# A quarter of a projection step behind the transposes in two attention slots, a whole step ahead of them in the third

## The chip, the cores and the metric

The kernel runs on one core of a Trainium2 chip. The metric is device time in microseconds (us) for one execution, and the number compared is the median over several executions. All data are float32.

## The reference, cut to what matters

Two layers follow each other on x of shape (16, 256, 512), with a condition of shape (16, 512). Each has a residual connection.

```python
# layer 1: adaptive norm, then attention with 16 heads of 32
scale, shift = split(cond @ W_emb + b_emb)
xn = rms_norm(x, g_norm) * (1 + scale) + shift
q, k, v = split_heads(xn @ W_qkv)              # 512 -> 3 * 512
q, k = rms_norm(q, g_q), rms_norm(k, g_k)
o = softmax(q @ k.T * 32 ** -0.5) @ v          # for each of 16 heads
x = x + o + o @ W_out
# layer 2: a GRU over the 256 time steps, started from cond
x = x + gru(x, h0=cond, W_ih, W_hh, b_ih, b_hh)
```

The change touches the attention of layer 1 only, and no arithmetic in it.

## The kernel before, in words

The program is unrolled. First come the weights and the projections of batch 0, then attention for 16 batches, then 256 steps of the GRU. An attention batch is worked off in four **slots**, one for each group of four heads. `slot0` to `slot3` run for batches 0 to 14, so that each of them runs 15 times. Batch 15 has a function of its own, `last_batch`, without projections.

A slot is a software pipeline over three things: the logits and softmax of the current group `w`, the transposes and the product with v of the previous group `prev`, and, spread over the four slots, all projections of the next batch `m = b + 1`. The names in the code and in the profile go like this:

- `logits` (L312, tile `lg`): 8 matmuls into four PSUM banks `lg0` to `lg3`, one bank a head.
- `project(b, n, s, ks, a)` (L244, tile `qkv`): one of q, k, v (s = 0, 1, 2) for one half of the tokens (n). It sums over four **steps** k. A step is four matmuls, j = 0 to 3. The matmul j has 32 columns of stationary operand (32 tokens) and writes 32 of the 128 partitions of the bank `a`; the moving operand is always the same 512 columns of the weights. In the trace each of these float32 matmuls stands as two records, one behind the other, so that a step is 8 records of PE.
- `maxima` (L328, DVE), `exps` (L334, ACT), `normalize` (L342 on DVE, L345 on POOL): the softmax of `w`. `exps` reads the four `lg` banks.
- `turn(prev)` (L218, tile `tpa`): 32 transposes of the previous group's attention weights, back into the four `lg` banks as soon as `exps` has read them.
- `put_turned(prev, "vava")` (L374, tile `attnT`): the copies of these four banks into SBUF, two by DVE and two by ACT in turn.
- `weigh(prev, bank)` (L391, tile `o`): 8 matmuls, four heads i for each of two halves k of the keys. Head i writes partitions 32 i to 32 i + 31. Heads 0 and 1 need the first two copies, heads 2 and 3 the other two.
- `turn_x` (L218, `tpx`), in slot 0, and `turn_qk` (L218, `tpqk`), twice in slot 3: transposes of the same shape as `tpa`, 16 each. `turn_qk` goes into the banks Z and Y.
- `norm_qk` (L273, DVE, tile `qkn`), `put_qk` (L296 on DVE, L294 on ACT), `put_v` (L267, ACT), `put_weighed` (L402, tile `oT`, ACT).

Under `manual_schedule` PE, DVE, ACT and POOL run their instructions in the order in which the code issues them. What sets the times is this order on each engine, with semaphores between the engines. So the place of a `project` call in a slot's code is its place in PE's queue. On PE, the four slots before the change are:

```
slot 0: logits, 4 steps, tpx, tpa, 2 steps, o
slot 1: logits, 5 steps, tpa, 1 step, o
slot 2: logits, 5 steps, tpa, 1 step, o
slot 3: logits, 4 steps, tpqk, tpa, tpqk, 2 steps, o
```

In slot 3 the first `tpqk` goes into the banks Z and Y, which hold q and k of the other half of the tokens until `norm_qk(m, 1, ...)` on DVE has read them; that follows the slot's `maxima` on DVE.

Of the kernel before, what the change touches and what calls it, by code (L numbers as in the profile page):

```python
# [19 lines left out]
def kernel(  # L20
# [125 lines left out]
    def tile_ps(name, bank, shape=(P, D)):  # L146
        pool = ps if len(bank) == 1 else ps_lg
        return pool.tile(list(shape), F32, tag=bank, name=name)
# [31 lines left out]
    def norm_first(b, parts=range(NT)):  # L180
        if parts[0] == 0:
            batches[b].ssx = small.tile([P, NT], F32, tag="ssx", name=f"ssx_{b}")
            batches[b].rs = Rsqrt(batches[b].ssx, D, NT, f"x{b}")
            if b != 2:
                batches[b].xs = p1.tile([P, NT, D], F32, tag="xs", name=f"xs_{b}")
        for n in parts:

            squares = batches[b].xs[:, n, :] if b != 2 else spare(f"squares_{n}")
            nc.scalar.activation(
                squares, x_tiles[b][:, n, :], AF.Square,  # L190
                accum_out=batches[b].ssx[:, n : n + 1],
            )
# [42 lines left out]
            else:  # L235
                nc.vector.tensor_scalar(dst, tps[r][:, c], a, s, ALU.mult, ALU.add)  # L236

    def project(b, n, s, ks, a):

        if isinstance(a, str):  # L240
            a = tile_ps(f"qkv_{b}_{n}_{s}", a)
        for k in ks:
            for j in range(4):
                nc.tensor.matmul(  # L244
                    a[32 * j : 32 * j + 32, :],
                    batches[b].xnT[:, k, n * P + 32 * j : n * P + 32 * j + 32],
                    wq[:, k, s * D : (s + 1) * D],
                    start=(k == 0),
                    stop=(k == KC - 1),
                )  # L250
        return a
# [17 lines left out]
    def norm_qk(b, n, accs, rstd):  # L269
        out = []  # L270
        for s in range(2):
            qk = p1.tile([P, H, DH], F32, tag="qkn", name=f"qkn_{b}_{n}_{s}", bufs=4)
            nc.vector.tensor_tensor(  # L273
                qk,
                accs[s].rearrange("p (h d) -> p h d", d=DH),
                rstd[:, s * H : (s + 1) * H].unsqueeze(2).to_broadcast([P, H, DH]),
                ALU.mult,
            )
            out.append(qk.rearrange("p h d -> p (h d)"))
        return out  # L280

    def turn_qk(b, n, normed, banks):
        tps = [tile_ps(f"tpqk_{b}_{n}_{r}", banks[r], (P, 2, NG, QR)) for r in range(R)]
        for s in range(2):
            for c in range(NG):
                turn_block([tp[:, s, c, :] for tp in tps], normed[s][:, c * P : (c + 1) * P])
        return tps
# [38 lines left out]
    def maxima(w, heads):  # L326
        for i in heads:
            nc.vector.tensor_reduce(w.neg[:, i, :], w.lg[i], AX.X, ALU.max, negate=True)  # L328

    def exps(w, heads):  # L330
        for i in heads:
            a = p1.tile([P, NT, T], F32, tag="attn", name=f"attn_{w.b}_{w.g}_{i}", bufs=8)
            for n in range(NT):
                nc.scalar.activation(  # L334
                    a[:, n, :], w.lg[i][:, n, :], AF.Exp,
                    bias=w.neg[:, i, n : n + 1], accum_out=w.den[:, i, n : n + 1],
                )
            w.attn[i] = a

    def normalize(w, heads=range(HG), engine=nc.gpsimd):  # L340
        r = slice(heads[0], heads[-1] + 1)
        nc.vector.reciprocal(w.rden[:, r, :], w.den[:, r, :])  # L342
        for i in heads:
            for n in range(NT):
                engine.tensor_scalar(  # L345
                    w.attn[i][:, n, :], w.attn[i][:, n, :], w.rden[:, i, n : n + 1], 1.0,
                    ALU.mult, ALU.mult,
                )
# [15 lines left out]
    def turn(w, banks=("lg0", "lg1", "lg2", "lg3")):  # L364

        if w is None:
            return
        for pair in range(HG // R):
            turn_pair(w, pair, banks[R * pair : R * pair + R])

    def put_turned_bank(w, i, engine):
        h, r = i // R * R, i % R
        dst = w.attnT[:, h : h + R].rearrange("p h k (n r c) -> p h k n r c", n=NT, r=R)[:, :, :, :, r]
        (nc.scalar.copy if engine is nc.scalar else nc.vector.tensor_copy)(dst, w.turned[i])  # L374

    def put_turned(w, engines):

        if w is None:
            return
        for i, e in enumerate(engines):  # L380
            put_turned_bank(w, i, nc.scalar if e == "a" else nc.vector)

    def weigh(w, bank):
        if w is None:
            return
        v = batches[w.b].v
        w.o = tile_ps(f"o_{w.b}_{w.g}", bank, (P, T))
        for k in range(NT):
            for i in range(HG):
                h = w.g * HG + i  # L390
                nc.tensor.matmul(  # L391
                    w.o[i * DH : (i + 1) * DH, :],
                    v[:, k, h * DH : (h + 1) * DH],
                    w.attnT[:, i, k, :],
                    start=(k == 0),
                    stop=(k == NT - 1),
                )

    def put_weighed(w, engine=nc.scalar):
        if w is None:  # L400
            return
        (nc.scalar.copy if engine is nc.scalar else nc.vector.tensor_copy)(oT[:, w.g, :, w.b], w.o)  # L402
# [56 lines left out]
    def slot1(b, w, prev, st):  # L459
        m = b + 1  # L460
        project(m, 0, 1, (2, 3), st.k)
        st.q1 = project(m, 1, 0, (0, 1, 2), "Z")
        maxima(w, range(HG))
        exps(w, range(HG))
        sq = st.s0.square(1, st.k)
        turn(prev)
        put_turned(prev, "vava")
        project(m, 1, 0, (3,), st.q1)
        st.s0.add(1, sq)
        if b + 3 < B:  # L470
            norm_first(b + 3, (0,))
        st.s0.rs.first()
        st.s1 = Stats(m, 1)
        st.sq = st.s1.square(0, st.q1)
        weigh(prev, "Y")
        put_weighed(prev)
        st.rstd = st.s0.rs.second()
        normalize(w)

    def slot2(b, w, prev, st):  # L480
        m = b + 1
        k = project(m, 1, 1, range(KC), "Y")
        maxima(w, range(HG))
        st.qk0 = norm_qk(m, 0, (st.q, st.k), st.rstd)
        st.v0 = project(m, 0, 2, (0,), "A")
        exps(w, range(HG))
        st.s1.add(0, st.sq)
        sq = st.s1.square(1, k)
        turn(prev)
        put_turned(prev, "vava")  # L490
        project(m, 0, 2, (1,), st.v0)
        st.s1.add(1, sq)
        if b + 3 < B:
            norm_first(b + 3, (1,))
        st.s1.rs.first()
        if b + 3 < B:
            batches[b + 3].rs.first()
        weigh(prev, "X")
        put_weighed(prev)
        if b == 0:  # L500

            for c in range(KC):
                d = wo[:, c, c * P : (c + 1) * P]
                nc.vector.tensor_tensor(d, d, ident, ALU.add)
            load_small()
        elif b == 2:
            for i in range(2):
                a = b_rows[:, 2 * i, :]
                nc.vector.tensor_tensor(a, a, b_more[:, i, :], ALU.add)
        st.accs = (st.q1, k)  # L510
        st.rstd = st.s1.rs.second()
        normalize(w)

    def slot3(b, w, prev, st):
        m = b + 1
        project(m, 0, 2, (2, 3), st.v0)
        st.v1 = project(m, 1, 2, (0, 1), "X")
        maxima(w, range(HG))
        qk1 = norm_qk(m, 1, st.accs, st.rstd)
        tq0 = turn_qk(m, 0, st.qk0, "ZY")  # L520
        if b + 3 < B:
            rstd = batches[b + 3].rs.second()
        exps(w, range(HG))
        put_qk(0, 0, tq0, nc.vector)
        put_qk(0, 1, tq0, nc.scalar)
        put_v(m, 0, st.v0)
        turn(prev)
        put_turned(prev, "vava")
        tq1 = turn_qk(m, 1, qk1, "ZY")
        project(m, 1, 2, (2, 3), st.v1)  # L530
        put_qk(1, 0, tq1, nc.vector)
        put_qk(1, 1, tq1, nc.scalar)
        if b + 3 < B:
            norm_apply(b + 3, rstd)
        normalize(w)
        weigh(prev, "A")
        put_weighed(prev)
        if m == B - 1:
            put_v(m, 1, st.v1)
# [89 lines left out]
    with tc.manual_schedule(engines=ORDERED):  # L629

        nc.scalar.preload_act_table_set("natural_log_exp_and_others")
        st = Batch()
# [236 lines left out]
    with tc.manual_schedule(engines=ORDERED):  # L869
# [7 lines left out]
        for c in (slice(0, 2 * B), slice(2 * B, TI * B)):  # L877
            for i, o in enumerate(first):
                a = xTs[0][:, 2 * i : 2 * i + 2].rearrange("p q t b -> p q (t b)")[:, :, c]
# [8 lines left out]
        for t in range(T):  # L888
            tl = t % TG
            p, s = divmod(t, 2)  # L890
# [18 lines left out]
            n = tile_of("n")  # L909
# [80 lines left out]
```

## Time and profile before

| what | value |
|---|---|
| median of 3 executions (lowest, highest) | 1746.63 us (1745.31, 1748.65) |
| the profiled execution's own time | 1746.58 us |
| its span, first to last instruction | 1744.8 us |
| granted TensorE clock, mean | 0.994 |
| PE busy | 1728.0 us, 99% of the span |
| DVE, ACT, POOL busy | 1051.4, 740.3, 315.5 us |
| projections L244 on PE | 354.7 us busy, 3072 records of 596 ns on average |
| slot 2 (236.87 to 245.56 us) | 8.69 us, PE busy 8.69 |
| slot 3 (245.56 to 255.63 us) | 10.07 us, PE busy 10.06 |
| slot 0 (255.63 to 264.74 us) | 9.11 us, PE busy 9.11 |
| slot 1 (264.74 to 273.49 us) | 8.75 us, PE busy 8.75 |

The last four rows are stretches of the trace from one slot's first projection to the next slot's. They are four consecutive slots in the middle of the attention part. A record of PE begins when the array takes the matmul, but its end is modelled and overlaps the next ones, so a "busy" PE can hold waits: what is read below are starts, and the length of a group of records from its first start to its last end. PEld is the loading of stationary operands, which runs beside the matmuls.

### The profile page before, as it was taken

The page shows a single profiled execution, that of the slowest core. Times are in us where ns is not written, and L with a number is a line of the kernel's source. Part 1 is how long each engine was busy: PE and PEld are TensorE (multiplying, and loading weights), DVE is VectorE, ACT ScalarE, POOL GpSimd, SP SyncE. Part 2 cuts the span into 40 slices and gives each one's busy share as a digit, 9 for nine tenths or more (in the row PEclk, how much of TensorE's full clock was granted, in tenths as well). Part 3 has the DMA queues.
Part 4 walks back from the last instruction along what each step waited for, and adds up shares of the span by engine and source line. Part 5 has one row for each costly group of instructions (what it writes and reads, how often), then busy time and mean ns, then how long its engine had stood idle before and what let it go on. Part 6 is the DMA issues. An engine that isn't in the chain of part 4 may idle for free.

```text
span 1744.8 us, 95656 instructions
## 1 busy us (share of the span) xinstructions
PE 1728.0 (99%) x42866; PEld 1272.0 (73%) x42866; DVE 1051.4 (60%) x3312; ACT 740.3 (42%) x2694; POOL 315.5 (18%) x773
## 2 busy tenths in 40 slices
PE   8999999999999999999999999999999999999998
PEld 4444444444444589888888888888888888888886
DVE  4777777777776645555555555555555555555554
ACT  4777777777777722222222222222222222222222
POOL 0443344334433410000000000000000000000000
PEclk9999999999999899999999999999999999999999
DMA  9100000000000310000000000000000000000000
GB/s 281 46 14 14 14 26 14 14 14 14 14 2 2 74 28 22 16 17 22 23 16 16 23 22 17 16 22 23 16 16 22 23 16 17 16 10 11 10 17 15
DMA packets 50506, 44.37 MB, mean 25 GB/s; under 512 B 10195, under 2 KB 43327, under 8 KB 50095
## 3 DMA queue, kind: packets, MB, share of 16 engines
q1 hardware_dynamic: 49959, 38.21, 8.3%
q8 instruction: 336, 5.51, 1.3%
q14 instruction: 75, 0.61, 0.1%
q10 hardware_dynamic: 136, 0.04, 0.0%
HBM read 29.79 MB, written 8.39 MB: 22 GB/s over the span
## 4 chain that ended last, share of the span: by engine, by line
PE 95%; DVE 2%; ACT 1%; issue 1%; DMA 0%; POOL 0%; SPq 0%; DVEq 0%; ACTq 0%
PE gr L808 25%; PE qkv L244 19%; PE gz L808 18%; PE gn L808 13%; PE o L765 6%; PE lg L312 4%; PE tpa L218 4%; PE o L391 4%; PE tpqk L218 1%; ACT attn L334 1%; PE tpx L218 0%; PE first L550 0%; DVE trh L831 0%; DMA we<-in_L_cond_W_emb_dram 0%; ACT n L912 0%
## 5 line engine op out<-in xcount | busy, mean ns | idle before, releaser
L244 PE MATMUL qkv<-wq,xnT 128*32 128x512 f32 x3072 | 354.7, 596 | 1.1 <-DVE xnT L236 1.1
L345 POOL TENSOR_SCALAR attn<-attn,rden 128x256 f32<-128x256 f32 x510 | 232.8, 478 | 379.0 <-DVE rden L342 275.2
L906 ACT ACTIVATE r<-trr 128x64 f32<-128x64 f32 x256 | 65.4, 256 | 514.8 <-DVE trr L831 512.8
L808 PE MATMUL gr<-wih,xT 128*32 128x256 f32 x4096 | 268.4, 379 | 0.0
L334 ACT ACTIVATE attn<-lg,neg 128x256 f32<-128x256 f32 x512 | 234.4, 483 | 66.6 <-DVE neg L328 42.6
L831 DVE STREAM_TRANSPOSE trr<-gr 128x128 f32<-128x128 f32 x256 | 81.1, 317 | 274.6 <-PE gr L808 274.6
L244 PEld LDWEIGHTS qkv<-wq,xnT 128*32 128x32 f32 x3072 | 88.3, 109 | 182.1 <-issue 157.2
L912 ACT ACTIVATE n<-n 128x64 f32<-128x64 f32 x256 | 65.6, 256 | 308.6 <-DVE n L911 305.6
L808 PEld LDWEIGHTS gr<-wih,xT 128*32 128x32 f32 x4096 | 135.4, 110 | 82.3
L328 DVE TENSOR_REDUCE neg<-lg 128x2 f32<-128x512 f32 x256 | 159.2, 683 | 48.4 <-PE lg L312 48.2
L831 DVE STREAM_TRANSPOSE trh<-gn 128x128 f32<-128x128 f32 x256 | 81.1, 317 | 116.9 <-PE gn L808 116.9
L765 PE MATMUL o<-oT,wo 128*32 128x256 f32 x1920 | 147.8, 379 | 0.0
L808 PE MATMUL gr<-whh,padded 128*32 128x128 f32 x4096 | 135.9, 273 | 2.9 <-DVE padded L940 1.7
L942 POOL TENSOR_TENSOR y<-xT,padded 128x64 f32<-128x64 f32 x128 | 41.0, 320 | 535.3 <-DVE padded L940 535.3
L808 PEld LDWEIGHTS gr<-whh,padded 128*32 128x32 f32 x4096 | 115.0, 110 | 30.3 <-DVE padded L940 29.4
L808 PE MATMUL gz<-wih,xT 128*32 128x128 f32 x4096 | 135.5, 273 | 0.0
L808 PE MATMUL gz<-whh,padded 128*32 128x128 f32 x4096 | 135.5, 273 | 0.0
L808 PE MATMUL gn<-whh,padded 128*32 128x128 f32 x4096 | 135.5, 273 | 0.0
L808 PE MATMUL gr<-whh,h 128*16 128x128 f32 x4064 | 134.6, 273 | 0.4
L808 PE MATMUL gn<-whh,h 128*16 128x128 f32 x4064 | 134.5, 273 | 0.0
L808 PE MATMUL gz<-whh,h 128*16 128x128 f32 x4064 | 134.4, 273 | 0.0
L808 PEld LDWEIGHTS gz<-wih,xT 128*32 128x32 f32 x4096 | 117.8, 110 | 21.2
(119 smaller groups left out, 2499.8 us busy)
## 6 DMA issues: line engine op xcount, KB each, us to landing
x<-in_x_dram SPq DMA_DIRECT2D x16, 512.0 KB, 3.6
xin<-in_x_dram SPq DMA_DIRECT2D x256, 32.0 KB, 1.9
out_dram<-osb SPq DMA_DIRECT2D x248, 32.0 KB, 1.8
wq<-in_L_cond_W_qkv_dram SPq DMA_DIRECT2D x4, 768.0 KB
wih<-in_L_cond_W_ih_dram SPq DMA_DIRECT2D x16, 192.0 KB, 6.9
whh<-in_L_cond_W_hh_dram SPq DMA_DIRECT2D x16, 192.0 KB, 6.4
we<-in_L_cond_W_emb_dram SPq DMA_DIRECT2D x4, 512.0 KB, 4.9
wo<-in_L_cond_W_out_dram SPq DMA_DIRECT2D x1, 1024.0 KB, 17.8
```

The costliest lines, as they stand in the source:

```text
L218: nc.tensor.transpose(dst[r], src[q], ident[q, q])
L244: nc.tensor.matmul(a[32 * j : 32 * j + 32, :], batches[b].xnT[:, k, n * P + 32 * j : n * P + 32 * j + 32], wq[:, k, s * D : (s + 1) * D], ...
L312: nc.tensor.matmul(w.lg[i][:, n, :], qT[r, g, n * P : (n + 1) * P], kT[r, g, :], start=True, stop=True,)
L328: nc.vector.tensor_reduce(w.neg[:, i, :], w.lg[i], AX.X, ALU.max, negate=True)
L334: nc.scalar.activation(a[:, n, :], w.lg[i][:, n, :], AF.Exp, bias=w.neg[:, i, n : n + 1], accum_out=w.den[:, i, n : n + 1],)
L345: engine.tensor_scalar(w.attn[i][:, n, :], w.attn[i][:, n, :], w.rden[:, i, n : n + 1], 1.0, ALU.mult, ALU.mult,)
L391: nc.tensor.matmul(w.o[i * DH : (i + 1) * DH, :], v[:, k, h * DH : (h + 1) * DH], w.attnT[:, i, k, :], start=(k == 0), stop=(k == NT - 1),)
L765: nc.tensor.matmul(acc[32 * j : 32 * j + 32, :], w[:, k, P * j + 32 * m : P * j + 32 * m + 32], rhs, start=(k == 0), stop=(k == KC - 1),)
L808: nc.tensor.matmul(dst[32 * j : 32 * j + rows], stationary, w[:, k, :].rearrange("p (g j c) -> p j g c", g=3, c=P)[:, j, first::2][:, : ds ...
L831: nc.vector.transpose(tr.rearrange("p q s b -> p (q s b)"), gate)
L906: nc.scalar.activation(r, turned("r", t, gr[:, 0, :])[:, :, s, :], AF.Sigmoid)
L912: nc.scalar.activation(n, n, AF.Tanh)
```

## The change: what it does

`project` gets a list of the j's. In slots 1 and 2, the last step ahead of `turn(prev)` keeps its matmuls j = 0, 1, 2, and its matmul j = 3 is issued behind the transposes, right ahead of the whole step that already stood there. In slot 3, step 2 of `v1` moves from behind the second `turn_qk` to the front of the slot.

```diff
-    def project(b, n, s, ks, a):
+    def project(b, n, s, ks, a, js=range(4)):
...
         for k in ks:
-            for j in range(4):
+            for j in js:
...
     def slot1(b, w, prev, st):
         m = b + 1
         project(m, 0, 1, (2, 3), st.k)
-        st.q1 = project(m, 1, 0, (0, 1, 2), "Z")
+        st.q1 = project(m, 1, 0, (0, 1), "Z")
+        project(m, 1, 0, (2,), st.q1, (0, 1, 2))
         maxima(w, range(HG))
         exps(w, range(HG))
         sq = st.s0.square(1, st.k)
         turn(prev)
         put_turned(prev, "vava")
+        project(m, 1, 0, (2,), st.q1, (3,))
         project(m, 1, 0, (3,), st.q1)
...
     def slot2(b, w, prev, st):
...
-        st.v0 = project(m, 0, 2, (0,), "A")
+        st.v0 = project(m, 0, 2, (0,), "A", (0, 1, 2))
         exps(w, range(HG))
...
         put_turned(prev, "vava")
+        project(m, 0, 2, (0,), st.v0, (3,))
         project(m, 0, 2, (1,), st.v0)
...
     def slot3(b, w, prev, st):
         m = b + 1
         project(m, 0, 2, (2, 3), st.v0)
-        st.v1 = project(m, 1, 2, (0, 1), "X")
+        st.v1 = project(m, 1, 2, (0, 1, 2), "X")
         maxima(w, range(HG))
...
         tq1 = turn_qk(m, 1, qk1, "ZY")
-        project(m, 1, 2, (2, 3), st.v1)
+        project(m, 1, 2, (3,), st.v1)
```

## The prediction

> **What bounds the kernel now.** I read the page's busy times first, then the busy time of each engine in the stretches of four consecutive slots (slot 2, slot 3, slot 0, slot 1), then PE's records in order of time through the same slots, then the other engines around the places where PE's groups are too long.
>
> ```profile
> PE 1728.0 (99%) x42866; PEld 1272.0 (73%) x42866; DVE 1051.4 (60%) x3312; ACT 740.3 (42%) x2694; POOL 315.5 (18%) x773
> ```
>
> PE has no idle time to give back that this row could show. But its ends are modelled, so waits hide inside the groups. They come out when equal groups have unequal lengths. In PE's timeline (start, length, what, number of records):
>
> ```profile
> 243.33 1.22 PE L391 MATMUL o<-attnT,v 128*32 128x256 f32 x16
> ...
> 245.56 3.64 PE L244 MATMUL qkv<-wq,xnT 128*32 128x512 f32 x32
> 249.13 0.96 PE L218 MATMUL tpqk<-ident,qkn 64*128 64x64 f32 x16
> 249.87 1.21 PE L218 MATMUL tpa<-ident,attn 64*128 64x64 f32 x32
> 251.10 0.81 PE L218 MATMUL tpqk<-ident,qkn 64*128 64x64 f32 x16
> 251.83 1.92 PE L244 MATMUL qkv<-wq,xnT 128*32 128x512 f32 x16
> 253.57 1.05 PE L391 MATMUL o<-attnT,v 128*32 128x256 f32 x16
> ...
> 259.20 0.71 PE L218 MATMUL tpx<-ident,xs 64*128 64x64 f32 x16
> 259.75 1.27 PE L218 MATMUL tpa<-ident,attn 64*128 64x64 f32 x32
> 260.94 1.92 PE L244 MATMUL qkv<-wq,xnT 128*32 128x512 f32 x16
> 262.68 1.05 PE L391 MATMUL o<-attnT,v 128*32 128x256 f32 x16
> ...
> 264.74 4.50 PE L244 MATMUL qkv<-wq,xnT 128*32 128x512 f32 x40
> 269.17 1.21 PE L218 MATMUL tpa<-ident,attn 64*128 64x64 f32 x32
> 270.31 1.07 PE L244 MATMUL qkv<-wq,xnT 128*32 128x512 f32 x8
> 271.19 1.27 PE L391 MATMUL o<-attnT,v 128*32 128x256 f32 x16
> ```
>
> Three readings. First, a projection step costs 0.86 us: five steps take 4.50 and four 3.64; two take 1.92 and one 1.07. Second, `o` takes 1.05 us in slots 3 and 0, which have two steps behind the transposes, but 1.27 in slot 1 and 1.22 in slot 2, which have one: waits of 0.22 and 0.17 us. They belong to the copies of the transposes. In slot 1:
>
> ```profile
> 269.97 1.29 DVE L374 COPY attnT<-tpa 128x512 f32<-128x512 f32 x2 [2.66 <-ACT sq L258]
> 270.00 1.07 ACT L374 COPY attnT<-tpa 128x512 f32<-128x512 f32 x2 [0.15 <-PE tpa L218]
> ```
>
> DVE's second copy ends at 271.26, and `o` began at 271.19: heads 0 and 1 start, heads 2 and 3 wait. Third, in slot 3 the first `tpqk` takes 0.96 us where the `tpx` of slot 0, 16 transposes of the same shape, takes 0.71: 0.25 us. Its second bank is held by the second `qkn` product of DVE (the two run from 248.05 to 249.33).
>
> **How a step uses the array.** This decides the case. PE's timeline cut to 0.02 us (270.31 to 270.33) already holds all four matmuls of a step, and their second records follow at 270.76. So the four run beside each other, each in its own 32 columns of the array. In two passes of 0.43 us each such column group is filled for the whole 0.86 us. The wait in slot 1 shows what a partly filled array does:
>
> ```profile
> 270.76 0.61 PE L244 MATMUL qkv<-wq,xnT 128*32 128x512 f32 x4
> 271.19 0.39 PE L391 MATMUL o<-attnT,v 128*32 128x256 f32 x2
> ```
>
> From 271.20 to 271.39 only the two matmuls of heads 0 and 1 are on. In the record starts their second pass comes 0.215 us after the first, exactly as where all four heads run ((1.05 - 0.38) / 3 = 0.22, for four passes whose records are 0.38 long). Half the groups are not twice as fast. A quarter of a step should therefore take a whole step's time, in its group, while the other three groups go on.
>
> **The change, part by part.** Nothing is added or removed: the same matmuls, no DMA moved. PE's instruction sequence shows the moves as written (11 matmuls ahead and 5 behind in place of 12 and 4), and no semaphore wait on the lone matmul.
>
> Ahead of the transposes in slots 1 and 2: three matmuls in place of four save nothing but the fourth's start, at most 0.02 us / 3, taken as 0.01, since the transposes wait for two passes either way. The Trainium skill has a rule that speaks against the change here: "TensorE: Matmul & The Clock Gate", Part 3, "Measured speedup vs the span model", puts a pack of tiles at one matmul's time plus some 4 ns for each further tile. By it the saving ahead would be 0.004 us; no term changes.
>
> Behind the transposes: group 3 now has the lone matmul (2 passes) and its part of the whole step (2 passes), so 4 x 0.43 before its head of `o` can start. Groups 0 to 2 have 2 passes. The next `logits` come 0.31 us after the last start of `o`, which is one 0.22 us pass and 0.09 for the change of shape. They use all columns, so they wait for group 3. The stretch thus becomes that of a slot with two steps behind (slots 0 and 3), which is in the trace: +0.86 us, and `o` of 1.05, because the copies are done by then. So slot 1 gains 0.86 - 0.22 = +0.64, slot 2 0.86 - 0.17 = +0.69. Off this come small terms: the lone matmul leads, so group 3 starts 0.02 earlier than as fourth; the 0.01 above; and 0.02 once, since slot 2's first step waits for ACT's `oT` copy (its weight load sat idle 0.35 against 0.33 elsewhere), which has more time now. Together -0.03 in each slot. The same page's list "What overlaps and what doesn't" (Part 3, "The mechanism") holds matmuls to be strictly in program order. The starts here show groups 0 and 1 a pass ahead of 2 and 3 in `o`. With strict order the tail would still be group 3's four passes, so the sum stays.
>
> Who else is late: `sq` of q1 (ACT) and `put_weighed` follow the later matmuls, but the next thing to need them is the next slot's first step, 1.1 us after `logits` begin; ACT's two instructions (0.58 and 0.59) fit.
>
> Slot 3: 0.86 us more ahead, 0.86 less behind, so only waits count. The first `tpqk` would begin at 249.99, after `qkn` is done (249.33): 0.71 in place of 0.96. The `tpa` behind it started ahead of time by 0.05 in the long version, so from the start of `tpqk` to the end of `tpa` 1.95 us become 0.55 + 1.21 = 1.76: a gain of 0.19 (with slot 0's `tpa` of 1.27, which waits for the last `exps`, it would be 0.13). The second `tpqk` waits for `tpa`'s own end by its semaphores, so it moves with it. Then one step in place of two covers the copies. `tpqk` ends 0.61 later than before (0.86 - 0.25). ACT's row of `put_qk`, `put_v` and two `attnT` copies runs without a gap from 250.13 to 252.41 and moves by 0.55 (at 250.13 it left `exps`, not PE): 252.96. DVE's `attnT` ends at 252.15 + 0.61 = 252.76. `o` would start at 253.57 - 0.19 = 253.38. The cover holds with 0.4 us to spare, less some 0.14 us from a copy's end to the waiting matmul. So -0.19.
>
> Per batch: 0.64 + 0.69 - 0.06 - 0.19 = +1.08 us. Fifteen batches: +16.2 us. The profiled execution took 1746.58 us (1.8 more than its span of 1744.8), equal to the median of 1746.63. Forecast 1746.6 + 16.2 = 1762.8 us. GRU and start are untouched.
>
> **Bounds.** Of the lone quarter no row exists. From below: a quarter of a step, 0.215; from above 0.86 as a full step. I take the upper, since the two-group passes of `o` are the nearest row. Slot 3 lies between no gain (0) and -0.35 (0.25, and the second `tpqk`'s 0.81 also down to 0.71): 1760.4 to 1765.7.
>
> **Rivals.**
> 1. Faster: the matmuls of a step take turns, so a quarter is 0.215 us wherever it stands. Then PE's work ahead shrinks by as much as it grows behind, and the waits of 0.22 and 0.17 are filled: -0.215 - 0.17 - 0.19 = -0.575, times 15 = -8.6, so 1738. For it: this size fits the two waits just so. Against: four starts within 0.02 us, and equal passes with two and four groups. It decides if the lone quarter costs under 0.32 us: even with no saving ahead, two of them then cost less than the 0.39 + 0.06 + 0.19 that the waits and small terms give.
> 2. In between: a group that runs alone goes twice as fast, 0.43 for the lone matmul. Per batch 0.21 + 0.26 - 0.06 - 0.19 = +0.22, so +3.3: 1749.9. Against: the two-group passes again.
> 3. Slot 3's wait moves instead of going: `o` waits for `attnT` with one step as cover, and nothing is won there. 15 x 1.27 = 19.1: 1765.7. For it: ACT's row has no gap. Against: the 0.26 us left.
>
> That the change doesn't do what it says is excluded by the instruction sequence, in which the scheduler kept the order.
>
> **How the numbers follow.** Main case 0.78, rival 3 0.13, rival 2 0.04, rival 1 0.05. What a measurement of this kernel can tell from no change is 0.2%, 3.5 us. Rival 1 gives faster 0.05; rival 2 falls within: 0.04; slower 0.91. The range takes slot 3's bounds and rival 3, and some 2 us below for passes of group 3 that I have not seen: 1758 to 1767.
>
> **What would show it.** In slots 1 and 2: `tpa` to `logits` as in slot 0, `o` and the projection group ahead of it together 0.6 to 0.7 us longer, slots of about 9.35 us each (8.75 and 8.69 before). Slot 3: first `tpqk` 0.71, slot 9.87 us. I am wrong if slots 1 and 2 keep their length (then rival 1), if they grow by 0.2 (rival 2), or if slot 3's `o` is longer than 1.05 (rival 3).

## The result, and the profile after

The changed kernel takes 1760.9 us (median of 5 executions, 1759.53 to 1762.5). The kernel before took 1745.31 us (5 executions beside it, 1743.48 to 1748.65). The ratio is 1.0086, with a 95% interval of 1.0074 to 1.0099: 15.6 us slower, where +16.2 was forecast. (The forecast 1762.8 us is 1.9 us above the measured time; 1.3 of these lie in the kernel before, which the forecast put at 1746.6 us.) The profiled execution took 1760.24 us, with a span of 1758.5.

The page, first PE's busy time and then the projections' group (busy us, mean ns of a record):

```profile
PE 1740.3 (99%) x42866; PEld 1277.6 (73%) x42866; DVE 1051.6 (60%) x3312; ACT 745.2 (42%) x2694; POOL 317.2 (18%) x773
...
L244 PE MATMUL qkv<-wq,xnT 128*32 128x512 f32 x3072 | 379.6, 596 | 1.1 <-DVE xnT L236 1.1
```

The same 3072 records of 596 ns now cover 379.6 us in place of 354.7, that is 24.9 us more. Thirty lone quarters at 0.86 us would be 25.8. So the work is the same, but less of it lies side by side. The ends of the records are modelled, so this is a rough count; it is the first sign that a quarter alone is as long as a whole step.

The stretches of four consecutive slots (slot 2, slot 3, slot 0, slot 1), from one slot's first projection to the next slot's:

```profile
243.11:252.45 9.34, 9.34 (x116) 4.22 (x113) 7.09 (x16) 7.49 (x26) 3.72 (x9) 1.00 0.01 4
252.45:262.32 9.87, 9.81 (x149) 4.97 (x145) 7.83 (x18) 7.73 (x25) 3.79 (x9) 1.00 0.01 2
262.32:271.44 9.12, 9.12 (x132) 4.34 (x129) 7.02 (x16) 5.90 (x21) 2.93 (x8) 1.00 0.17 59
271.44:280.78 9.34, 9.34 (x117) 4.14 (x113) 5.23 (x12) 7.58 (x25) 4.24 (x10) 1.00 0.01 2
```

Slot 2 went from 8.69 to 9.34 us, slot 1 from 8.75 to 9.34, and slot 3 from 10.07 to 9.87. PE's timeline through slot 3 and slot 1 shows why:

```profile
252.45 4.50 PE L244 MATMUL qkv<-wq,xnT 128*32 128x512 f32 x40
256.88 0.72 PE L218 MATMUL tpqk<-ident,qkn 64*128 64x64 f32 x16
257.43 1.16 PE L218 MATMUL tpa<-ident,attn 64*128 64x64 f32 x32
258.65 0.80 PE L218 MATMUL tpqk<-ident,qkn 64*128 64x64 f32 x16
...
260.27 1.05 PE L391 MATMUL o<-attnT,v 128*32 128x256 f32 x16
...
271.44 4.49 PE L244 MATMUL qkv<-wq,xnT 128*32 128x512 f32 x38
275.86 1.21 PE L218 MATMUL tpa<-ident,attn 64*128 64x64 f32 x32
277.00 1.48 PE L244 MATMUL qkv<-wq,xnT 128*32 128x512 f32 x9
277.89 0.80 PE L391 MATMUL o<-attnT,v 128*32 128x256 f32 x6
278.31 0.59 PE L244 MATMUL qkv<-wq,xnT 128*32 128x512 f32 x1
278.32 1.45 PE L391 MATMUL o<-attnT,v 128*32 128x256 f32 x10
```

The other engines in the same two slots, where the text below needs them:

```profile
258.03 0.47 ACT L294 ACTIVATE kT<-tpqk,gk_col 128x256 f32<-128x256 f32 x1
...
258.86 1.10 ACT L374 COPY attnT<-tpa 128x512 f32<-128x512 f32 x2
...
276.66 1.29 DVE L374 COPY attnT<-tpa 128x512 f32<-128x512 f32 x2 [2.65 <-ACT sq L258]
```

- Slot 3: the first `tpqk` takes 0.72 us in place of 0.96, and `o` still takes 1.05 with only one step as cover: ACT's copies end at 259.96, 0.31 us before `o` begins.
- Slot 1, ahead of the transposes: 38 records in place of 40 take 4.49 us in place of 4.50. Two records fewer saved 0.01 us.
- Slot 1, behind them: the records of the projections start at 277.00 (four), 277.46 (four), 277.89 (one) and 278.31 (one). The single ones are the two passes of a whole step that column group 3 still has to do, while the other groups are done. Two heads of `o` begin at 277.89 and a third at 278.10, before group 3 is through. Head 3 follows at 278.74, and `o` ends at 279.77.
- The third head, head 2, comes 0.21 us behind the first two, and 0.15 us after DVE's second copy ends (277.95). So the wait for the copies still stands in `o`, but the late group 3 covers it: it no longer adds to the slot.

For the experiments I use the length of a slot from its first `logits` record to the next slot's, as a median over the 15 slots of a kind. Before, slots 0 to 3 take 9.112, 8.729, 8.692 and 10.066 us; in the changed kernel 9.122, 9.337, 9.340 and 9.868. Summed over all 60 slots, the changed kernel is 16.1 us longer. The rest of the program, which the change leaves alone, takes between 1189.9 and 1195.5 us in the nine profiled executions of this document, so the sum of the slots is the sharper measure, and the times with their intervals are the check on it. Each sum below lies in the interval of its time.

### The profile page after: what moved, and what is told of

Its sections match the earlier page's. It is cut to its first block, busy times and chain, and to the rows that moved or that the text cites. A ratio compares the mean times of both kernels' runs of the same rounds, so it can differ in the third digit from the quotient of the medians.

```text
span 1758.5 us, 95656 instructions
## 1 busy us (share of the span) xinstructions
PE 1740.3 (99%) x42866; PEld 1277.6 (73%) x42866; DVE 1051.6 (60%) x3312; ACT 745.2 (42%) x2694; POOL 317.2 (18%) x773
## 4 chain that ended last, share of the span: by engine, by line
PE 95%; DVE 2%; ACT 1%; issue 1%; DMA 0%; POOL 0%; SPq 0%; DVEq 0%; ACTq 0%
PE gr L811 25%; PE qkv L244 19%; PE gz L811 18%; PE gn L811 13%; PE o L768 6%; PE o L391 4%; PE lg L312 4%; PE tpa L218 4%; PE tpqk L218 1%; ACT attn L334 1%; PE tpx L218 0%; PE first L553 0%; DMA we<-in_L_cond_W_emb_dram 0%; DVE trh L834 0%; ACT n L915 0%
## 5 line engine op out<-in xcount | busy, mean ns | idle before, releaser
L244 PE MATMUL qkv<-wq,xnT 128*32 128x512 f32 x3072 | 379.6, 596 | 1.1 <-DVE xnT L236 1.1
L244 PEld LDWEIGHTS qkv<-wq,xnT 128*32 128x32 f32 x3072 | 94.3, 109 | 199.9 <-issue 175.2
```

The lines of the kernel that those rows point to most:

```text
L244: nc.tensor.matmul(a[32 * j : 32 * j + 32, :], batches[b].xnT[:, k, n * P + 32 * j : n * P + 32 * j + 32], wq[:, k, s * D : (s + 1) * D], ...
```

## The experiments

Each diff is against the kernel before, cut to the lines that matter; `...` stands for lines left out. The times of the kernel before are medians of the executions beside the run: 1745.92 us for the first four, 1745.54 for the last three.

### The two parts apart

Slot 3 alone:

```diff
-        st.v1 = project(m, 1, 2, (0, 1), "X")
+        st.v1 = project(m, 1, 2, (0, 1, 2), "X")
...
-        project(m, 1, 2, (2, 3), st.v1)
+        project(m, 1, 2, (3,), st.v1)
```

> Only the move in slot 3 (one projection step to the front), slots 1 and 2 as before. Theory (the first tpqk no longer waits for DVE's second qkn product): slot 3 goes from 10.07 to 9.87 us, its first tpqk from 0.96 to 0.71, o stays 1.05: 15 x -0.20 = -3.0 us. Rival (the wait moves to o, whose cover is one step shorter): slot 3 keeps 10.07, o gets 0.2 longer, 0 us.

Measured: 1742.47 us, ratio 0.9979 (0.9968 to 0.999), -3.5 us. Slot 3 takes 9.872 us, the others as before; the slots' sum is 2.9 us shorter. The wait for DVE's `qkn` is gone and none took its place.

The quarters alone:

```diff
-        st.q1 = project(m, 1, 0, (0, 1, 2), "Z")
+        st.q1 = project(m, 1, 0, (0, 1), "Z")
+        project(m, 1, 0, (2,), st.q1, (0, 1, 2))
...
+        project(m, 1, 0, (2,), st.q1, (3,))
         project(m, 1, 0, (3,), st.q1)
...
-        st.v0 = project(m, 0, 2, (0,), "A")
+        st.v0 = project(m, 0, 2, (0,), "A", (0, 1, 2))
...
+        project(m, 0, 2, (0,), st.v0, (3,))
         project(m, 0, 2, (1,), st.v0)
```

> Only the quarters in slots 1 and 2, slot 3 as before. Theory (the lone matmul costs its column group a whole step, and logits wait for that group): slots 1 and 2 go to 9.34 us as with the whole change, 15 x (0.61 + 0.65) = +18.9 us. Rival (part of the loss is an effect of slot 3's move on the other slots): less than +17 us.

Measured: 1768.76 us, ratio 1.0127 (1.0108 to 1.0146), +22.8 us. Slots 1 and 2 take 9.337 and 9.340 us, exactly as in the whole change, and slot 3 takes 10.070. The slots' sum is 18.9 us longer. The median shows 3.9 us more than the slots; in the profiled execution 1.8 us of it lie ahead of the first `logits` (35.4 us after the start in place of 33.5), where nothing was changed and the granted clock of the first 33 us is 0.90 in place of 1.00. Where the rest lies is not shown. The two parts do not touch each other: -2.9 and +18.9 make +16.0, and both together gave +16.1.

### Does the price go with the number of late matmuls?

Two of the four matmuls are moved behind, j = 2 and 3, with slot 3's move as in the change:

```diff
-        st.q1 = project(m, 1, 0, (0, 1, 2), "Z")
+        st.q1 = project(m, 1, 0, (0, 1), "Z")
+        project(m, 1, 0, (2,), st.q1, (0, 1))
...
+        project(m, 1, 0, (2,), st.q1, (2, 3))
         project(m, 1, 0, (3,), st.q1)
```

and the same in slot 2.

> The whole change, but half a step is moved behind the transposes in slots 1 and 2: matmuls j = 2 and 3 in place of j = 3 alone. Theory (the column groups work beside each other, the latest one sets the end): as with the changed kernel, slots 1 and 2 at 9.34 us, +16 us against the kernel before. Rival (a matmul that stands apart takes time of its own, so the price goes with their number): twice the price of slots 1 and 2, 15 x (2 x 1.26 - 0.20) = +35 us; or, if the matmuls of a step take turns, two quarters of 0.215 more, about +22 us.

Measured: 1762.41 us, ratio 1.0097 (1.0079 to 1.0115), +16.5 us. Slots 1 and 2 take 9.337 and 9.340 us, to the nanosecond those of one late matmul. PE's timeline behind the transposes of a slot:

```profile
250.08 1.48 PE L244 MATMUL qkv<-wq,xnT 128*32 128x512 f32 x10
250.98 0.60 PE L391 MATMUL o<-attnT,v 128*32 128x256 f32 x4
251.39 0.60 PE L244 MATMUL qkv<-wq,xnT 128*32 128x512 f32 x2
251.41 1.45 PE L391 MATMUL o<-attnT,v 128*32 128x256 f32 x12
```

Now two heads of `o` go early (4 records) and two groups are late. The stretch has the same marks as with one late group: from 250.08 to the late passes at 251.39 is 1.31 us, and in the changed kernel it is 1.31 too (277.00 to 278.31). Two late matmuls cost nothing more than one. That rules out that the matmuls take turns, and it rules out a price for each.

### A quarter in another cut

All four matmuls of the step stay ahead with 384 of their 512 moving columns, and all four do the last 128 columns behind the transposes. Slot 3's move is as in the change. `project` takes the columns `c`; only the first part of a step k = 0 starts the accumulation:

```diff
-        st.q1 = project(m, 1, 0, (0, 1, 2), "Z")
+        st.q1 = project(m, 1, 0, (0, 1), "Z")
+        project(m, 1, 0, (2,), st.q1, slice(0, D - 128))
...
+        project(m, 1, 0, (2,), st.q1, slice(D - 128, D))
         project(m, 1, 0, (3,), st.q1)
```

and the same in slot 2.

> A quarter of the step moved in another cut: all four matmuls of the step stay ahead with their first 384 of 512 columns, and all four do their last 128 columns behind the transposes (slots 1 and 2); slot 3's move as in the change. Theory (all four groups share the moved work, two passes of 0.11 us each): 0.215 us leaves the front and fills the waits of 0.22 and 0.17 us in o: slots 1 and 2 at 8.51 and 8.52 us, with slot 3's -0.20 together -0.59 x 15 = -8.8 us. Rival (the wait only moves ahead, since tpa comes 0.2 us earlier to the lg banks that exps still reads, or the four added matmuls cost as much as they fill): slots 1 and 2 keep 8.73 and 8.69, -3 us in all.

Measured: 1739.59 us, ratio 0.9964 (0.9952 to 0.9977), -6.3 us. Slots 1 and 2 take 8.517 and 8.528 us; the slots' sum is 8.1 us shorter. PE's timeline (line numbers from there on are one higher in this kernel):

```profile
225.84 4.29 PE L244 MATMUL qkv<-wq,xnT 128*32 128x512 f32 x40
230.05 1.21 PE L218 MATMUL tpa<-ident,attn 64*128 64x64 f32 x32
231.19 1.28 PE L244 MATMUL qkv<-wq,xnT 128*32 128x128 f32 x16
232.29 1.05 PE L392 MATMUL o<-attnT,v 128*32 128x256 f32 x16
```

Here 0.21 us did leave the front (4.29 in place of 4.50), 0.21 came behind (1.28 in place of 1.07), and `o` fell to 1.05, without a wait. This is a quarter of a step that costs a quarter of a step: it is cut across all four column groups. The kernel is faster than the one before and the changed one. Against slot 3's move alone the time's intervals overlap; there the slots decide (8.52 and 8.53 against 8.73 and 8.69).

### How much can go behind

Twice the columns (256 of 512):

```diff
-        st.q1 = project(m, 1, 0, (0, 1, 2), "Z")
+        st.q1 = project(m, 1, 0, (0, 1), "Z")
+        project(m, 1, 0, (2,), st.q1, slice(0, D - 256))
...
+        project(m, 1, 0, (2,), st.q1, slice(D - 256, D))
         project(m, 1, 0, (3,), st.q1)
```

and the same in slot 2, with slot 3's move.

> As the run that moves the last 128 columns of all four matmuls behind the transposes, but the last 256. Theory (0.43 us leaves the front; o's waits of 0.22 and 0.17 are filled already by half of it; tpa's second half has about 0.4 us to spare before the last exps): slots 1 and 2 within 0.1 us above 8.51 and 8.52, so -6 to -8.8 us. Rival (each added matmul costs time of its own in proportion to columns, or the waits grow at once): 8.7 us and more, -3 us.

Measured: 1742.65 us, ratio 0.9982 (0.9973 to 0.9992), -2.9 us; the slots' sum is 3.3 us shorter. Slots 1 and 2 take 8.686 and 8.682 us: nearly what they took before, so nearly all of what the cover had won is lost again. The theory, 8.61 and 8.62 us at most, was wrong, and the rival's total (8.7, -3) was met. PE's timeline in slot 2 tells which half of the rival it was:

```profile
235.92 4.07 PE L244 MATMUL qkv<-wq,xnT 128*32 128x512 f32 x40
239.92 1.38 PE L218 MATMUL tpa<-ident,attn 64*128 64x64 f32 x32
241.24 1.50 PE L244 MATMUL qkv<-wq,xnT 128*32 128x256 f32 x16
242.55 1.05 PE L392 MATMUL o<-attnT,v 128*32 128x256 f32 x16
```

As much left the front as came behind, 0.43 us each, and `o` waits no more, but `tpa` takes 1.38 us in place of 1.21. The columns cost only their length; a wait of 0.17 us has moved to the transposes.

A whole step, all four matmuls:

```diff
-        st.q1 = project(m, 1, 0, (0, 1, 2), "Z")
+        st.q1 = project(m, 1, 0, (0, 1), "Z")
...
-        project(m, 1, 0, (3,), st.q1)
+        project(m, 1, 0, (2, 3), st.q1)
```

and the same in slot 2, with slot 3's move.

> A whole step (all four matmuls, all columns) moved behind the transposes in slots 1 and 2, slot 3's move as in the change: four steps ahead of tpa, two behind. Theory: o no longer waits (0.22 and 0.17 us won), but tpa comes 0.86 us earlier to banks that exps holds until some 0.1 us after tpa's present start; its second half, 0.5 us later, has about 0.4 us to spare, so it waits about 0.46: slots 1 and 2 at 8.97 and 8.98 us, with slot 3 (-0.20) together +0.33 x 15 = +5 us. Rival (the step ahead covers nothing): slots 1 and 2 at 8.51 and 8.52, -8.8 us.

Measured: 1756.87 us, ratio 1.0056 (1.0042 to 1.0069), +11.3 us; the slots' sum is 9.4 us longer. Slots 1 and 2 take 9.109 and 9.110 us. The timeline of PE and ACT shows the wait that the step had covered:

```profile
238.20 0.77 PE L218 MATMUL tpa<-ident,attn 64*128 64x64 f32 x17
...
238.66 0.50 ACT L334 ACTIVATE attn<-lg,neg 128x256 f32<-128x256 f32 x1
...
239.02 0.24 ACT L334 ACTIVATION_READ_ACCUMULATOR attn<-lg,neg 128x1 f32 x1
...
239.31 0.71 PE L218 MATMUL tpa<-ident,attn 64*128 64x64 f32 x15 [0.34 <-ACT attn L334]
```

Seventeen transposes run. The other fifteen wait for the last `exps` to leave its bank. As a median over slots 1 and 2 the last transpose starts 6.24 us after the slot's first `logits`, both here and with 256 columns behind. Before, it started at 6.50 in slot 1 and 6.51 in slot 2. So only some 0.26 us could leave the front at all, where I had reckoned with 0.4. The 128 columns took 0.21 of it, which is why they fit and 256 did not.

### What the cover in slot 3 is worth

Both late steps of `v1` to the front of slot 3, slots 1 and 2 as before:

```diff
-        st.v1 = project(m, 1, 2, (0, 1), "X")
+        st.v1 = project(m, 1, 2, range(KC), "X")
...
-        project(m, 1, 2, (2, 3), st.v1)
```

> Slots 1 and 2 as before; in slot 3 both late steps of v1 are moved to the front, none is left behind the second tpqk. Theory (the first tpqk has no wait left to win, and the copies of attnT on ACT end at about 253.95 on the time scale of the trace before, 0.14 us later heads 2 and 3 can start, where o could begin at 253.35): slot 3 is 0.5 us longer than before, 10.6 us, +7.8 us. Rival (the cover behind the transposes is not needed in slot 3): slot 3 at 9.87 us, -3 us.

Measured: 1754.3 us, ratio 1.0046 (1.003 to 1.0061), +8.8 us. Slot 3 takes 10.470 us, 0.40 more than before; the slots' sum is 6.1 us longer. PE's timeline, and then ACT's:

```profile
255.68 1.54 PE L391 MATMUL o<-attnT,v 128*32 128x256 f32 x16
```

```profile
255.02 1.09 ACT L374 COPY attnT<-tpa 128x512 f32<-128x512 f32 x2
```

ACT's copies end at 256.11, `o` had begun at 255.68 and takes 1.54 us in place of 1.05. One step in front is won, and the second one is needed behind.

## Why the prediction was right

- **A step fills its column groups for 0.86 us, and a lone quarter costs its group a whole step.** Shown. One late matmul and two late matmuls give the same slots. Forecast were +0.61 and +0.66 us for slots 1 and 2 (0.64 and 0.69, less 0.03); they are +0.608 and +0.648. The upper bound, 0.86, was the right end to take, and the two-group passes of `o` were the row to take it from. The changed kernel shows it for a single group as well: group 3's records start 0.43 us apart (277.46, 277.89, 278.31), like those of a full step, and the last three passes of head 3, alone in the array, 0.22 us apart. The small terms were added up wrongly: by their own list they are 0.08 us a batch (twice 0.02 and 0.01, and 0.02 once), not 0.06. Measured, slots 1 and 2 stay 0.03 and 0.04 below 0.64 and 0.69, 0.07 together.
- **The waits of 0.22 and 0.17 us in `o` go.** They no longer add to the slots, but what that gave back is less than what the late group takes. In slot 1 head 2 still waits for its copy, 0.21 us, while the slot waits for group 3; the prediction had reckoned that the copies were done by then, which holds for head 3 alone. The cut by columns gives the same waits back without the late group.
- **`logits` wait for the late group.** They begin 0.31 us after the last start of `o` here as before.
- **Slot 3: -0.19.** Measured -0.198 with the whole change and -0.194 alone. That the sum is so close is in part luck. From the start of the first `tpqk` to the end of `tpa` it is 1.71 us, where 1.76 was forecast: `tpa` takes 1.16. But the second `tpqk`, which was to move with that end, starts 0.06 us after it, where it was 0.02 before (251.10 after 251.08). It also starts 0.15 us after the last `kT` copy out of the banks Z and Y (258.50; before, 0.13 after 250.97). Which of the two it waits for was not tested. The copies kept 0.31 us of cover, where 0.4 was forecast: ACT's row began 0.64 us later in the slot, not 0.55. Without any step as cover slot 3 is 0.40 us longer than before.
- **Slot 0: 0.** It grew by 0.010 us in the whole change alone, 0.15 us in all. No run tells why.
- **Rivals.** Rival 1 (turns) would have given slots 1 and 2 shorter by 0.2, rival 2 longer by 0.2; both grew by over 0.6. Rival 3 (slot 3's wait moves to `o`) fell with `o` at 1.05, and with slot 3 measured alone.

The sum per batch was 1.08 us, and the slots give 16.1 / 15 = 1.07. Where my expectations missed was in the later runs: the room ahead of `exps` is 0.26 us, not 0.4 (the whole step cost slots 1 and 2 0.38 and 0.42 in place of 0.24 and 0.29), and slot 3 without cover cost 0.40 in place of 0.50.

## What to carry to other kernels

Where matmuls run beside each other in column groups, as these float32 matmuls of 32 stationary columns do, "a quarter of the work" is a quarter only if it is cut across all groups; one group's share on its own is as long as the whole. Before filling a wait with work from ahead of it, look at what that work covers where it stands: here 0.26 us could go and 0.43 could not. And read waits of a saturated engine from the unequal lengths of equal groups, since its busy share will not show them.

## What the runs showed that I had not expected

The best amount to move is narrow. Moving 0, 0.21, 0.43 and 0.86 us of a step behind the transposes, cut across all groups, gives slot 1 lengths of 8.729, 8.517, 8.686 and 9.109 us: one wait ends and another begins within a quarter of a microsecond.

PE's records also start out of the program's order by more than the prediction had read from `o`. In the changed kernel six records of `o` start from 277.89 on, ahead of the projection record of 278.31, the second pass of a matmul that stands before all of them in the program. Each head has two matmuls of two passes. Heads 0 to 2 start the first pass of their second matmul at 278.32, 278.33 and 278.53, and head 3 starts its first matmul, which stands ahead of these in the program, at 278.74. So the strict order that the prediction weighs against its sum does not hold between column groups here. Groups that have nothing to wait for run on; the sum was the same either way, as the late group sets the end.
